# Steps of two layers moved by a slot, dummy matmuls added, and an int4 maximum taken on TensorE, in a four-layer kernel on one core

## The chip, the cores and the metric

The kernel runs on one NeuronCore of a Trainium2 chip. One launch computes all four layers. The metric is the device time of one execution in microseconds. Shorter is better. The core has a matrix engine (PE in the profile, with its weight loads as PEld), a vector engine (DVE), a scalar engine (ACT), a general engine (POOL) and a queue engine (SP) that issues DMAs. Each engine works through its own queue in program order, and semaphores tie the queues together.

## The reference, cut to what matters

The input is 4096 tokens of 128 numbers (16 sequences of 256). Each of four layers normalises x and adds an attention and a feed-forward part of the normalised rows to x.

```python
# layer 0: attention over the 76 keys of highest importance; 8 experts of 512 tokens each
Q, K, V = heads(xn @ wq.T + bq), heads(xn @ wk.T + bk), heads(xn @ wv.T + bv)   # 16 heads of 8
importance = relu(xn @ wi1.T + bi1) @ wi2.T + bi2        # keys outside the top 76 are masked
attn0 = softmax(Q @ K.T / sqrt(8)) @ V @ wo.T + bo
scores = softmax(xn @ wg)                                 # every expert takes its 512 best tokens
top_scores, sel = top_k(scores.T, 512)
routed = xn[sel] * top_scores
ffn0 = scatter_add(sel, (silu(routed @ w1) * (routed @ w3)) @ w2)

# layer 1: sparse causal attention (16 heads of 64), and 8 experts, 2 for each token
# layer 2: attention in learned windows, and a ternary network of width 512
# layer 3: causal attention, 16 heads of 64, S = 256; an int4 linear part with a low-rank part
attn3 = softmax(q @ k.T / 8 + causal) @ v @ Wo + bo
scale = max(abs(kernel)) / 7
w = clip(round(kernel / scale), -8, 7) * scale
ffn3 = xn @ w + bias + (xn @ a) @ b
```

## The kernel before, in words

The 4096 tokens are eight chunks of 512 rows (NC = 8, CT = 512), held as tiles of 128 rows by 128 columns. The order of all instructions is written out by hand: the program is a row of *slots*, and a Python loop says which step of which chunk goes into which slot. A step is a function; a longer step is a generator, and every `yield` in it ends its part in that slot, so one more `yield` moves everything after it one slot later. There is no planner: what is written earlier is earlier in each engine's queue. An engine whose next instruction isn't ready stands still, whatever is behind it.

**PSUM.** The eight accumulator banks are fixed: `sc` is two buffers of two banks (scores, first products, projections), `tp` two single banks (transposes), `mm` and `po` one single bank each. In layer 0, `bank()` hands out `tp`, `tp`, `mm` in turn. A user of a bank waits until the user before has been copied out.

**Layer 0** (`Layer0.run`) has slots -8 to 67, eight for each chunk. In the even slots `exps` forms scores of queries and kept keys in both `sc` buffers on PE (L817), and ACT takes their exponentials (tile `a_p`, L823). In the odd slots `maxima` forms scores of the next chunk in both `sc` buffers (L783), and DVE reduces them (L789); `outputs` multiplies the exponentials of the slot before with the values (L834). `queries`, `divided`, `turned`, `project` and `value` are transposes and small products in between. `prelude` prepares a chunk two chunks ahead.

Beside them runs the routing. `choice` finds for every expert the gate value that keeps 512 tokens: a bitwise search of 15 rounds, one a slot from slot -2, in each of which DVE compares (L485), PE counts with matmuls (L491) and DVE picks. `warm(n)` puts n dummy matmuls of 128x256 in bfloat16 into PE's queue (L373), whose result nobody reads. `expert(e)` starts in slot 19 + 3e: one-hot places on DVE (two slots), indices on PE (`pix`), in the next slot their sums (`eighths`, L605) and four indirect DMAs on POOL that gather 128 rows each (L613), later the product with the gate on DVE (L623), transposes (L629), first products (L638, both `sc` buffers), second products (L648), the copy y on ACT (L653), and four indirect DMAs that add rows to memory (L662). After the last expert eight loads on SP fetch the sums (`fetch`), and POOL adds them to the attention's result (`finish`, L998).

From slot 57 on, `Route.early` normalises layer 0's results for layer 1: `stat` and `root` on DVE, `apply` on ACT and POOL, `turn` (transposes on PE, L1298, and a copy on ACT).

**Layers 1 and 3** share the class `Pipeline`. Its `slots` loop works on one pair of heads u in each slot (128 of them, 16 for a chunk): `scores`, `minima` on DVE, `exps` on ACT, `divide` on POOL (L1145), `transposes` (L1155), `values` (L1169), projections (L1082, L1095; copies on ACT, L1087), and `extra(u)`, a function of the layer. `out_half` is the output projection of 128 rows, nine products into the `mm` bank (L1185, L1187). In layer 3 `norm_steps` normalises the next chunk, beginning in the chunk's slot 3 and ending with four transposes into the `mm` bank (L1059) and a copy on ACT (L1061).

In layer 1 `extra` also carries the chain `route.last`, `route.places` (which place each row has), `scatter` (64 indirect DMAs on POOL), 36 lanes of `blocks` (expert products, L1498 and L1511, with weights gathered by indirect DMA), `gather`, and from slot 56 the generator `aside`, whose end is `quantized`: the int4 weights of layer 3, with the maximum over 128 x 128 numbers.

**Layer 2** (`Layer2.run`) is a loop over chunks with its calls written out; during its last turns `beside(n)` advances layer 3 by n slots.

Of the kernel before, what the change touches and what calls it, by code (L numbers as in the profile page):

```python
# [19 lines left out]
P = 128  # L20
D = 128
# [201 lines left out]
class Layer0:  # L223
# [245 lines left out]
    def choice(self):  # L469
# [9 lines left out]
        for i in range(15):  # L479
# [8 lines left out]
            self.warm(12 if i < 2 else 4)  # L488
# [81 lines left out]
    def expert(self, e):  # L570
# [32 lines left out]
        yield  # L603

# [14 lines left out]
        if e % 2 == 0:  # L619

            yield
# [18 lines left out]
        for hc, p1 in enumerate(p1s):  # L640
            sl = p2.tile([P, CAP], F32, tag="sl", name="sl")
            nc.scalar.activation(sl, p1[:, 0, :], AF.Silu)
            nc.vector.tensor_tensor(g[:, hc, :], p1[:, 1, :], sl, ALU.mult)
        yield
# [235 lines left out]
    def begin(self):  # L880
# [36 lines left out]
        for _ in lane:  # L917
# [6 lines left out]
            -8: [(self.stats, 6, 2, 6), (self.stats, 7, 2, 6), (self.root, 2, 6), (self.apply, 2), (self.apply, 3), warm],  # L924
# [8 lines left out]
    def run(self, tail):  # L933
# [8 lines left out]
        warm = {kk: 5 for kk in range(-8, 4)} | {kk: 2 for kk in range(12, 22)} | {kk: 3 for kk in range(53, 64)}  # L942
        loads = 19 + 3 * NE + 8
        for kk in range(-8, 8 * NC + 4):
# [4 lines left out]
            if 0 <= c < NC and r % 2 == 0:  # L949
                self.exps(c, r // 4, r // 2 % 2)  # L950
# [18 lines left out]
            if kk == 45:  # L969

                self.pg = self.k.po()
# [39 lines left out]
class Pipeline:  # L1011
# [25 lines left out]
    def norm_steps(self, c):  # L1037
# [12 lines left out]
        for t in range(TT):  # L1050
            nc.gpsimd.tensor_scalar(
                xn[:, t, :], x[:, t, :], mv[:, t, 0:1], y[:, t : t + 1], ALU.subtract, ALU.mult
            )
            if t == 1:
                yield
        yield
# [122 lines left out]
    def out_half(self, s, t, wo, first=None):  # L1179

        k, nc = self.k, self.k.nc
        p = k.mm1()
        if first is not None:
            t0 = s % 2 * S + t * P
            nc.tensor.matmul(p[:, :D], lhsT=self.xnT[s // 2][:, t0 : t0 + P], rhs=first, start=True, stop=False)  # L1185
        for n in range(8):
            nc.tensor.matmul(  # L1187
                p[:, :D], lhsT=self.oT[s][:, n, t * P : (t + 1) * P], rhs=wo[:, n, :],
                start=(first is None and n == 0), stop=(n == 7),
            )  # L1190
        return p[:, :D]

    def slots(self, extra, mid=None):

        if self.own:
            yield
            yield from self.norm_steps(0)
            yield
# [55 lines left out]
class Route:  # L1254
# [71 lines left out]
    def early(self):  # L1326

        at = {}
        for first, n in ((0, 2), (2, 2), (4, 2), (6, 1)):
            for c in range(first, first + n):  # L1330
                u = 57 + c + c // 6
                at.setdefault(u, []).append((self.stat, c, first, n))
                for late, step in ((0, self.apply), (1, self.turn)):
                    at.setdefault(59 + c + late, []).append((step, c))
# [6 lines left out]
    def last(self):  # L1341
# [5 lines left out]
        self.apply(c)  # L1347
        yield
# [203 lines left out]
def layer1(k, wk_, w, route, l2, aside, warm):  # L1552
# [15 lines left out]
    def extra(u):  # L1568
# [10 lines left out]
        for g, at, n in ((0, 15, 2), (1, 93, 2)):  # L1579
# [5 lines left out]
        if 0 <= u - 49 < NB // 2:  # L1585
            lanes.append(route.blocks(2 * (u - 49)))
# [26 lines left out]
class Layer2:  # L1613
# [266 lines left out]
    def run(self, wk_, att, begin, l3, route):  # L1880
# [20 lines left out]
        for n in range(NC + 1):  # L1901
# [39 lines left out]
            do(self.turn, q)  # L1941
            do(self.first, f, 3)
            beside(1)
# [27 lines left out]
def quantized(k, pool, a):  # L1971
# [10 lines left out]
    yield  # L1982
    mx = pool.tile([P, 1], F32, name="q_mx")
    nc.gpsimd.partition_all_reduce(mx, m, P, bass_isa.ReduceOp.max)
    yield
# [6 lines left out]
    q = pool.tile([P, D], F32, name="q_q")  # L1992
# [16 lines left out]
def layer3(k, wk_, sh, room, w, xs, out):  # L2009
# [10 lines left out]
    res = {}  # L2020

    def extra(u):
        for late, t in ((9, 0), (13, 1)):
            s, at = (u - late) // 8, (u - late) % 8
            if at or not 0 <= s < 2 * NC:
                continue
            c, n = s // 2, s % 2 * 2 + t
            if n == 0:
                res[c] = k.xp.tile([P, TT, D], F32, tag="x", name="res")
            p = pipe.out_half(s, t, w["o"], first=w["eff"])  # L2030
            nc.vector.tensor_tensor(res[c][:, n, :], p, w["bias"], ALU.add)
            nc.gpsimd.tensor_tensor(res[c][:, n, :], res[c][:, n, :], xs[c][:, n, :], ALU.add)
            if n == 3:
                nc.sync.dma_start(out[c * CT : (c + 1) * CT, :].rearrange("(t p) d -> p t d", p=P), res[c])

# [155 lines left out]
```

## Time and profile before

| what | value |
|---|---|
| median of 3 runs | 1945.82 us (1943.68 to 1952.15) |
| the profiled execution | 1939.03 us |
| its span, first to last instruction | 1937.3 us |
| its mean granted TensorE clock | 0.985 |
| layer 0 | from the start to about 366 us |
| layer 1 | to about 995 us |
| layer 2 | to about 1390 us |
| layer 3 | to the end |

The profile is one execution, recorded by the hardware. The first part of its page gives each engine's busy time, share of the span and number of instructions. The next cuts the span into 40 equal slices of 48.4 us, with one digit each for the busy tenths, and for the clock that PE was granted. A further part follows the chain of work that ended last, from the last instruction back, and gives its shares by engine. Groups and timelines show an instruction as engine, line, operation, output<-input by the program's names, shape and count; in brackets stands the idle time before it and what ended that. In the list of waits a line reads: engine, tile and line, what it waited for, the total in us, the number of times, the longest.

### The profile page before, as it was taken

Reading aid. Unit: us, or ns where it says so; the run is one execution under the profiler, and the core shown is the slowest. Engines: PE = TensorE matmul, PEld = TensorE weight load, DVE = VectorE, ACT = ScalarE, POOL = GpSimd, SP = SyncE. Lnnn points to the kernel's source line nnn. Section 1 sums busy time; section 2 is a strip of 40 time slices with the busy share of each in tenths; the row PEclk is TensorE's granted clock in tenths of the full one; section 3 lists DMA queues with packets and bytes.
Section 4 is the critical chain, followed back from the end, with each engine's and each line's share of the span. In section 5 each row is a group of like instructions: output and inputs, shape, how many; then the busy total and the mean of one; then the engine's idle time right before and its main releaser. Section 6 shows DMA issues by size and latency. Waiting matters only on the chain.

```text
span 1937.3 us, 39257 instructions
## 1 busy us (share of the span) xinstructions
PE 1850.1 (95%) x13823; PEld 1335.7 (69%) x13823; DVE 1226.1 (63%) x4819; ACT 1052.8 (54%) x3162; POOL 960.8 (50%) x1388
## 2 busy tenths in 40 slices
PE   9998889889999899999999999999999999999998
PEld 5555455568878788887754555555577877877786
DVE  6888664697665555568765555443277667766765
ACT  4334545656666566666644444444466666666664
POOL 4015776337997466565664444421144444444442
PEclk9989999899999999999999999999999999999999
DMA  8500223200014354300010000000000000000000
GB/s 248 145 1 13 30 30 66 74 1 23 33 34 129 101 140 136 88 20 15 16 41 5 9 10 12 12 1 1 1 1 8 1 7 7 7 1 7 7 1 12
DMA packets 83208, 72.28 MB, mean 37 GB/s; under 512 B 14466, under 2 KB 74020, under 8 KB 82852
## 3 DMA queue, kind: packets, MB, share of 16 engines
q1 hardware_dynamic: 66784, 38.01, 6.9%
q0 software_dynamic: 15488, 31.61, 6.7%
q8 instruction: 109, 1.79, 0.4%
q14 instruction: 87, 0.71, 0.1%
q10 hardware_dynamic: 740, 0.17, 0.0%
HBM read 49.70 MB, written 24.25 MB: 38 GB/s over the span
## 4 chain that ended last, share of the span: by engine, by line
PE 64%; DVE 7%; POOL 7%; issue 2%; ACT 1%; POOLq 0%; ACTq 0%; DVEq 0%
PE sc L1811 11%; PE sc L1082 9%; PE po L1169 7%; PE tp L1155 7%; PE sc L1110 7%; PE mm L1187 5%; PE sc L1095 4%; POOL e L1145 3%; POOL xb L1452 2%; DVE e L1125 2%; PE po L1511 2%; PE mm L1498 2%; PE mm L1851 2%; DVE eT L1156 1%; PE sc L1803 1%
## 5 line engine op out<-in xcount | busy, mean ns | idle before, releaser
L1145 POOL TENSOR_TENSOR e<-e,rs 128x256 f32<-128x256 f32 (+2 forms) x512 | 400.0, 807 | 483.1 <-DVE rs L1143 448.3
L1136 ACT ACTIVATE e<-e,mn 128x128 f32<-128x128 f32 (+2 forms) x1024 | 442.4, 434 | 285.8 <-DVE mn L1125 281.8
L1156 DVE COPY eT<-tp 128x384 f32<-128x384 f32 x512 | 261.3, 552 | 59.8 <-PE tp L1155 59.6
L1811 PE MATMUL sc<-ff,h 128*128 128x512 f32 x512 | 227.2, 593 | 1.6 <-DVE l_mn L1738 1.6
L1155 PE MATMUL tp<-ident,e 128*128 128x128 f32 x1536 | 219.0, 278 | 8.6 <-POOL e L1145 5.6
L1175 DVE COPY oT<-po 128x512 f32<-128x512 f32 x128 | 88.3, 690 | 215.8 <-PE po L1169 215.8
L1155 PEld LDWEIGHTS tp<-ident,e 128*128 128x128 f32 x1536 | 173.3, 141 | 61.6 <-issue 37.3
L1136 ACT ACTIVATION_READ_ACCUMULATOR e<-e,mn 128x1 f32 x1024 | 191.9, 187 | 0.0
L1811 PEld LDWEIGHTS sc<-ff,h 128*128 128x128 f32 x512 | 94.4, 190 | 106.4 <-issue 101.2
L1125 DVE CUSTOM_DVE_ANT_0 e<-sc,causal 128x128 f32<-128x128 f32 (+1 forms) x512 | 151.8, 353 | 11.2 <-PE sc L1110 10.8
L1125 DVE CUSTOM_DVE_ANT_0 e<-sc,sparse 128x128 f32<-128x128 f32 (+1 forms) x512 | 138.8, 328 | 7.2 <-POOL dist L183 2.2
L1082 PE MATMUL sc<-m,qkv 128*128 128x256 f32 x512 | 126.8, 390 | 1.7 <-DVE mn L1125 1.7
L1691 POOL TENSOR_SCALAR n<-dist,reach 128x128 f32<-128x128 f32 (+1 forms) x128 | 119.2, 931 | 16.4 <-DVE l_mn L1738 5.0
L1187 PE MATMUL mm<-out,oT 128*128 128x128 f32 x1024 | 124.9, 275 | 0.0
L1187 PEld LDWEIGHTS mm<-out,oT 128*128 128x128 f32 x1024 | 119.4, 192 | 0.1
L1790 POOL TENSOR_TENSOR x<-l_o,x 128x256 f32<-128x256 f32 x16 | 11.6, 727 | 199.7 <-DVE l_o L1784 199.3
L1082 PEld LDWEIGHTS sc<-m,qkv 128*128 128x128 f32 x512 | 92.5, 190 | 17.0 <-DVE mn L1125 2.3
L1110 PE MATMUL sc<-n 64*128 64x128 f32 (+1 forms) x1024 | 101.5, 337 | 1.3 <-ACT n L1087 0.8
L1169 PE MATMUL po<-eT,p_v 128*64 128x256 f32 (+1 forms) x1024 | 99.4, 333 | 2.0 <-DVE eT L1156 1.9
L1169 PE MATMUL po<-eT,m 128*64 128x256 f32 (+1 forms) x1024 | 98.1, 332 | 0.4 <-DVE eT L1156 0.4
L1169 PEld LDWEIGHTS po<-eT,p_v 128*64 128x64 f32 x1024 | 63.9, 136 | 43.7 <-issue 16.3
L1742 ACT ACTIVATE p_e<-p_e,l_mn 128x128 f32<-128x128 f32 (+1 forms) x128 | 56.3, 441 | 68.3 <-DVE l_mn L1738 68.1
(433 smaller groups left out, 3686.6 us busy)
## 6 DMA issues: line engine op xcount, KB each, us to landing
xb<-zero SPq DMA_DIRECT2D x1, 4608.0 KB, 20.4
xb<-xb SPq DMA_DIRECT2D x36, 128.0 KB, 2.8
yb<-yb SPq DMA_DIRECT2D x36, 128.0 KB, 2.3
x<-in_L_attn_x SPq DMA_DIRECT2D x8, 256.0 KB, 3.8
m<-in_L_ffn_w SPq DMA_DIRECT2D x8, 256.0 KB, 11.3
xn_d<-x SPq DMA_DIRECT2D x8, 256.0 KB, 8.0
m<-acc_d SPq DMA_DIRECT2D x8, 256.0 KB, 5.4
h<-in_L_ffn_h_wT SPq DMA_DIRECT2D x2, 1024.0 KB, 7.5
```

What stands on the lines that cost most here:

```text
L1082: nc.tensor.matmul(p[:, n, i * S : (i + 1) * S], lhsT=self.wqk[n][:, (2 * gg + i) * P : (2 * gg + i + 1) * P], rhs=(self.xk if n else self ...
L1110: nc.tensor.matmul(ps[:, j, c0:c1], lhsT=qk[r, 0, i, qt * P : (qt + 1) * P], rhs=qk[r, 1, i, k0 : k0 + c1 - c0], start=True, stop=True,)
L1125: nc.vector.tensor_tensor_reduce(out=e[:, j, c0:c1], in0=ps[:, j, c0:c1], in1=self.mask[:, c0:c1], scale=1.0, scalar=3e38, op0=ALU.add, op ...
L1136: nc.scalar.activation(e[:, j, c0:c1], e[:, j, c0:c1], AF.Exp, bias=mn[:, n], scale=-1.0, accum_out=sums[:, n])
L1145: nc.gpsimd.tensor_tensor(e[:, :, c0:c1], e[:, :, c0:c1], bcast(rs[:, 2 * qt : 2 * qt + 2], 2, c1 - c0), ALU.mult)
L1155: nc.tensor.transpose(pt[:, n * P : (n + 1) * P], e[:, j, c0 : c0 + P], k.ident)
L1156: nc.vector.tensor_copy(eT[:, j, :], pt[:, :384])
L1169: nc.tensor.matmul(o[64 * j : 64 * j + 64, t * P :], lhsT=v[:, t ^ self.swap, h : h + 64], rhs=eT[:, j, t * S : t * P + S], start=(t == 0) ...
L1175: nc.vector.tensor_copy(self.oT[s][:, 2 * gg : 2 * gg + 2, :].rearrange("p i s -> p (i s)"), self.po.pop(g))
L1187: nc.tensor.matmul(p[:, :D], lhsT=self.oT[s][:, n, t * P : (t + 1) * P], rhs=wo[:, n, :], start=(first is None and n == 0), stop=(n == 7),)
L1691: self.nc.gpsimd.tensor_scalar(mk[:, j, c0:c1], self.k.dist[:, c0:c1], reach[:, g, t : t + 1], 1e18, ALU.is_gt, ALU.mult)
L1811: self.nc.tensor.matmul(ph, lhsT=self.w[wh][:, c, m * P : (m + 1) * P], rhs=src[c], start=(c == 0), stop=(c == NF - 1))
```

## The change

- **Layer 0, dummies.** 25 instead of 3 in slot -8; in the search 28, 12 and then 7 a round instead of 12, 12 and then 4; 5 instead of 2 in slots 12 to 16.
- **Layer 0, order.** `exps` moves from the head of its slot to behind `project` and `value`. Odd experts take their index sums and gather one slot later, and all experts now have three slots from the gather to the product with the gate (odd ones had two). Second products come a slot later after the first. So an even expert ends one slot later and an odd one three. The loads of the sums leave three slots later. A bank of the dummies is taken in slot 47 instead of 45.
- **Layer 1's rows.** `turn` comes one slot later, for chunks 0 to 6 in layer 0's tail and for chunk 7 in `last`. Scatter, blocks and gather follow one slot later.
- **Layer 3.** `norm_steps` has one more `yield` ahead of its transposes; at the start one `yield` less stands before it. In layer 2 one `beside(1)` moves ahead of `first(f, 3)`. The sum with the bias and x is made on POOL first, for a whole chunk, and PE's result is added to it by DVE. Of the last sequence, seven of nine products of each half are done in slots 126 and 127, in the `mm` and a `tp` bank, and the last two in slot 128.
- **The int4 maximum.** POOL's reduction over the partitions gives way to a copy of each row's maximum to 128 columns (DVE), a transpose into the `mm` bank (PE) and a reduction along the row (DVE).

```diff
@@ Layer0.choice
-            self.warm(12 if i < 2 else 4)
+            self.warm((28, 12, 7)[min(i, 2)])
@@ Layer0.expert
         nc.scalar.activation(fourths, pix[:, :P], AF.Copy)
         yield
+        if e % 2:
+            yield
 
         nc.tensor.matmul(pix[:, P : P + 8], lhsT=fourths, rhs=self.eighths, start=True, stop=True)
...
         yield
         yield
-        if e % 2 == 0:
-
-            yield
+
+        yield
 
         nc.vector.tensor_tensor(
...
             nc.vector.tensor_tensor(g[:, hc, :], p1[:, 1, :], sl, ALU.mult)
+        yield
+
         yield
         py = self.bank()
@@ Layer0.begin
-            -8: [(self.stats, 6, 2, 6), (self.stats, 7, 2, 6), (self.root, 2, 6), (self.apply, 2), (self.apply, 3), warm],
+            -8: [(self.stats, 6, 2, 6), (self.stats, 7, 2, 6), (self.root, 2, 6), (self.apply, 2), (self.apply, 3), (self.warm, 25)],
@@ Layer0.run
-        warm = {kk: 5 for kk in range(-8, 4)} | {kk: 2 for kk in range(12, 22)} | {kk: 3 for kk in range(53, 64)}
-        loads = 19 + 3 * NE + 8
+        warm = {kk: 5 for kk in range(-8, 4)} | {kk: 5 for kk in range(12, 17)} | {kk: 2 for kk in range(17, 22)} | {kk: 3 for kk in range(53, 64)}
+        loads = 19 + 3 * NE + 11
...
-            if 0 <= c < NC and r % 2 == 0:
-                self.exps(c, r // 4, r // 2 % 2)
             if 0 <= c + 1 < NC and r % 2:
                 self.maxima(c + 1, r // 2)
...
             if r >= 6 and 0 <= c + 1 < NC:
                 self.value(c + 1, r - 6)
-            if kk == 45:
+            if 0 <= c < NC and r % 2 == 0:
+
+                self.exps(c, r // 4, r // 2 % 2)
+            if kk == 47:
@@ Pipeline.norm_steps
             if t == 1:
                 yield
+        yield
         yield
         pt = k.mm1()
@@ Pipeline.out_half
-    def out_half(self, s, t, wo, first=None):
+    def out_half(self, s, t, wo, first=None, p=None, upto=8):
...
-        for n in range(8):
+        for n in range(6, 8) if begun else range(upto):
@@ Pipeline.slots
         if self.own:
-            yield
             yield from self.norm_steps(0)
             yield
@@ Route.early
-                    at.setdefault(59 + c + late, []).append((step, c))
+                    at.setdefault(59 + c + 2 * late, []).append((step, c))
@@ Route.last
         self.apply(c)
+        yield
         yield
         self.turn(c)
@@ layer1
-        for g, at, n in ((0, 15, 2), (1, 93, 2)):
+        for g, at, n in ((0, 16, 2), (1, 94, 2)):
...
-        if 0 <= u - 49 < NB // 2:
-            lanes.append(route.blocks(2 * (u - 49)))
+        if 0 <= u - 50 < NB // 2:
+            lanes.append(route.blocks(2 * (u - 50)))
@@ Layer2.run
             do(self.turn, q)
+            beside(1)
             do(self.first, f, 3)
-            beside(1)
@@ quantized
+    q = pool.tile([P, D], F32, name="q_q")
+    nc.vector.tensor_copy(q, m.to_broadcast([P, D]))
+    yield
+    pm = k.mm1()
+    nc.tensor.transpose(pm[:, :P], q, k.ident)
     mx = pool.tile([P, 1], F32, name="q_mx")
-    nc.gpsimd.partition_all_reduce(mx, m, P, bass_isa.ReduceOp.max)
-    yield
+    nc.vector.tensor_reduce(mx, pm[:, :P], AX.X, ALU.max)
     yield
@@ layer3
+        if u == NU - 2:
+            last.append(k.mm1())
+        if u == NU - 1:
+            last.append(k.tp())
+        if u in (NU - 2, NU - 1):
+            pipe.out_half(2 * NC - 1, u - NU + 2, w["o"], first=w["eff"], p=last[-1], upto=6)
         for late, t in ((9, 0), (13, 1)):
             s, at = (u - late) // 8, (u - late) % 8
-            if at or not 0 <= s < 2 * NC:
+            if at or not 0 <= s < 2 * NC - 1:
                 continue
...
                 res[c] = k.xp.tile([P, TT, D], F32, tag="x", name="res")
+                nc.gpsimd.tensor_tensor(res[c], xs[c], bcast(w["bias"], 1, TT), ALU.add)
             p = pipe.out_half(s, t, w["o"], first=w["eff"])
-            nc.vector.tensor_tensor(res[c][:, n, :], p, w["bias"], ALU.add)
-            nc.gpsimd.tensor_tensor(res[c][:, n, :], res[c][:, n, :], xs[c][:, n, :], ALU.add)
+            nc.vector.tensor_tensor(res[c][:, n, :], p, res[c][:, n, :], ALU.add)
             if n == 3:
                 nc.sync.dma_start(out[c * CT : (c + 1) * CT, :].rearrange("(t p) d -> p t d", p=P), res[c])
+        if u == NU:
+            c = NC - 1
+            for t in range(2):
+                p = pipe.out_half(2 * NC - 1, t, w["o"], p=last[t])
+                nc.vector.tensor_tensor(res[c][:, 2 + t, :], p, res[c][:, 2 + t, :], ALU.add)
+            nc.sync.dma_start(out[c * CT : (c + 1) * CT, :].rearrange("(t p) d -> p t d", p=P), res[c])
```

More of the change, by code (lines that the diff above doesn't have):

```diff
@@ L6 @@
 import concourse.tile as tile
-from concourse import bass_isa, mybir
+from concourse import mybir
 from concourse.masks import make_identity
@@ L1177, in values @@
             )
-    def out_half(self, s, t, wo, first=None):
+    def out_half(self, s, t, wo, first=None, p=None, upto=8):
         k, nc = self.k, self.k.nc
-        p = k.mm1()
-        if first is not None:
+        begun = p is not None and upto == 8
+        if p is None:
+            p = k.mm1()
+        if first is not None and not begun:
             t0 = s % 2 * S + t * P
             nc.tensor.matmul(p[:, :D], lhsT=self.xnT[s // 2][:, t0 : t0 + P], rhs=first, start=True, stop=False)
-        for n in range(8):
+        for n in range(6, 8) if begun else range(upto):
             nc.tensor.matmul(
@@ L1991, in quantized @@
     yield
-    q = pool.tile([P, D], F32, name="q_q")
     nc.vector.tensor_scalar(q, kw, inv[:, 0:1], None, ALU.mult)
@@ L2019, in layer3 @@
     pipe = Pipeline(k, wk_, xs, (w["Wq"], w["Wk"]), w["Wv"], k.causal, home=home)
-    res = {}
+    res, last = {}, []
     def extra(u):
+        if u == NU - 2:
[4 more added lines that the diff above has]
+            pipe.out_half(2 * NC - 1, u - NU + 2, w["o"], first=w["eff"], p=last[-1], upto=6)
         for late, t in ((9, 0), (13, 1)):
             s, at = (u - late) // 8, (u - late) % 8
-            if at or not 0 <= s < 2 * NC:
+            if at or not 0 <= s < 2 * NC - 1:
                 continue
```

## The prediction

> **What bounds the kernel now.** I read the page first, then busy time by stretches, then the waits of the stage that loses most, then timelines around each edited place.
>
> ```profile
> PE 1850.1 (95%) x13823; PEld 1335.7 (69%) x13823; DVE 1226.1 (63%) x4819; ACT 1052.8 (54%) x3162; POOL 960.8 (50%) x1388
> PEclk9989999899999999999999999999999999999999
> PE 64%; DVE 7%; POOL 7%; issue 2%; ACT 1%; POOLq 0%; ACTq 0%; DVEq 0%
> ```
>
> PE is busy 95% of the span and holds 64% of the chain that ended last. So an edit pays only where PE is idle or runs at a reduced clock, and costs whatever it adds where PE is full. The clock dips only early. Busy time by stretches places the dips:
>
> ```profile
> 30.00:37.00 7.00, 4.97 (x22) 2.78 (x22) 6.42 (x28) 5.51 (x14) 2.97 (x5) 0.51 0.87 273
> 112.00:119.00 7.00, 7.00 (x45) 5.43 (x42) 3.77 (x11) 1.93 (x2) 0.00 (x0) 0.51 0.00 0
> 347.50:354.30 6.80, 6.78 (x41) 3.23 (x41) 5.94 (x35) 5.02 (x11) 2.07 (x3) 0.50 0.00 0
> 664.90:671.80 6.90, 4.76 (x22) 4.47 (x22) 3.42 (x6) 0.38 (x1) 5.28 (x8) 0.51 0.26 69
> ```
>
> After the stretch and its length come busy time of PE, weight loads, DVE, ACT and POOL, then the granted clock. Each of these runs at half clock, so it can return at most half its length, 3.4 us, and less where another engine is nearly full (DVE 6.42 of 7 in the first).
>
> **Start of layer 0, -1.0 us (-2 to 0).** The 22 added dummies before slot -7's transposes take 0.12 each (17 of them took 2.02 at 57 us), 2.6 us, and PE is idle 3.39 us there waiting for ACT's normalised rows, so they are covered. If they hold the clock in 30 to 37, ACT (5.51 of 7 busy) lets at most 1.5 through.
>
> **Search, -1.0 (-2.9 to +4.6).** Sixteen more dummies in the first round take 1.9 and lie in the 2.3 us that PE waits for DVE's comparison. Three more in 13 rounds cost 0.36 each where DVE waits for PE's count, which it does in 4 of the 15 rounds (4.3 us in all; DVE is busy 54.67 of the 64.5 us): 1.4, or 4.6 if all pay. If the clock holds in 112 to 119, DVE's 2.85 us below its rate of the stretch before (6.62 of 7) come back. I take a little over the middle. The 15 dummies of slots 12 to 16 are covered by DVE, busy 56.76 of 63 us there; without that cover they cost 1.8.
>
> **Experts, 183 to 326 us, -10 (-19 to 0).** The waits of this stage:
>
> ```profile
> ACT y L653 <- DMA acc_d<-y,ids: 11.4, 2, 6.7
> DVE xr L623 <- DMA xr<-xn_d,ids: 10.3, 3, 4.2
> PE sc L817 <- DVE g L643: 5.0, 7, 1.0
> ```
>
> ACT can't write y before the last expert's adds have landed, and what stands behind y on ACT waits too. Four gathers an expert (about 1.25 us each on POOL) and four adds with three memsets (7.5) share POOL's queue, behind the `pick` and `ka` operations. PE inherits these waits three times: 1.77 at 208 (eighths behind ACT), 2.69 at 248 (a bank held until y), 2.08 at 227 (a bank held until DVE, stuck on xr). An odd expert's gather a slot later and two slots more to its product, and second products and adds a slot later for all, put about 12 us (two slots of 6) between gather and use. I take back 6.5, and 3.4 for the two 3.4 us half-clock stretches that follow. The moved `exps`: after first products, PE waits about 1.5 us for the score banks, eight times. Now queries, quotients and projection (0.44 to 1.7 us) go first, hiding some 8 in all. Against it, `maxima` wants the same two banks and must wait for ACT's 1.93 us of exponentials with less work between: 1 us in eight pairs, -8 again. The end at -19 is the second without the bill; at 0 the waits only move.
>
> **Late layer 0, 326 to 366, +1 (-5 to +8).** `exps` last in its slot leaves ACT's 1.93 us bare before `outputs`: the 0.9 us of work moved ahead is lost in each of 8 pairs, 7. The early transposes one slot later remove the 1.34 us at 344.5 and most of the half-clock stretch behind it, together 4; 2 more by filling with expert products, which now end three slots later.
>
> ```profile
> 345.84 1.21 PE L1298 MATMUL tp<-ident,m 128*128 128x128 f32 x4 [1.34 <-ACT m L1292]
> ```
>
> This row shows a 1.34 us idle time, followed by the half clock from 347.5. The Trainium skill ("TensorE: Matmul & The Clock Gate", its table "Why this matters for your kernels") only warns of idle gaps over about 3 us; by that, no dummy or delay here would change the clock, and these terms would be the idle times alone. The row decides: short gaps among thin matmuls suffice.
>
> The eight fetches leave SP three slots later (SP has nothing else then); the first sums on POOL ended at 328 and DVE's statistics began at 335.5, and three slots of 2.3 us use that up: 0 to 3, inside the range.
>
> **Start of layer 1, +1.5 (-2.5 to +4).** PE waited 2.53 us for chunk 7's rows, and the scores after it began at 380.70, released by ACT's copy L1087. ACT is late through the normalisation ahead of it in its queue, which doesn't move. So the idle time stays, the transposes (0.6 at full clock) come later, and a longer idle time may keep the half clock for another 3.4 us. Scatter, blocks and gather move along one slot: nothing else waits.
>
> **The int4 maximum, -5.1 (-6.5 to -3).**
>
> ```profile
> 657.87 0.38 POOL L1984 PARTITION_ALL_REDUCE q_mx<-q_m  x1 [5.76 <-issue]
> 666.01 1.44 POOL L1145 TENSOR_TENSOR e<-e,rs 128x256 f32<-128x256 f32 x2 [7.77 <-issue]
> 666.67 0.47 PE L1155 MATMUL tp<-ident,e 128*128 128x128 f32 x1 [4.78 <-POOL e L1145]
> ```
>
> The operation takes 0.38, but POOL stands still 5.76 before and 7.77 after it without a releaser, around two pool reconfigurations. The division, and PE behind it, wait. The block products L1498 recur every 6.32 us; three periods from 652.57 took 25.09 instead of 18.97: 6.1 us lost, clock included. The replacement's copy and reduction are 0.3 each on DVE, which idles there; the transpose takes the single `mm` bank right after a block's product and waits for ACT to empty it, as L2003 does at 685 (0.5 to 0.7), then 0.3: 1.0. The Trainium skill ("GPSIMD Engine Reference", 4. When to use GPSIMD) calls POOL the only option for a reduction across partitions, which would rule this edit out and make the term 0. PE's own transposes (0.28 each) show that PE can turn the column.
>
> **Layer 2's call order, -1.4 (-1.5 to 0).** The layer 3 transposes now precede `first(f, 3)`, whose matmuls cover ACT's copy out of the `mm` bank:
>
> ```profile
> 1371.09 3.84 PE L1851 MATMUL mm<-f,ff 128*128 128x128 f32 x32 [1.41 <-ACT m L1061]
> ```
>
> **Layer 3's transposes, +4.5 (-5.2 to +8).** They move from the 9th to the 10th slot of a chunk.
>
> ```profile
> 1434.22 0.33 PE L1059 MATMUL mm<-ident,m 128*128 128x128 f32 x1 [0.29 <-POOL m L1051]
> ```
>
> The gain is clear: two waits for POOL, 0.74 us a chunk, 5.2 in seven. But `out_half` runs in that 10th slot and wants the same single bank. In ACT's queue the copy out of it then stands behind exponentials and L1087. In a plain pair (transposes at 1450.60) L1087 ends 4.68 us after the pair began; the copy adds 0.6, so `out_half` starts at about 5.35, against 4.71 now: 0.65 later in 7 chunks. The sum with the bias on POOL (1.25 for four times 0.45) holds DVE until about 1441.9 where its next operation starts at 1442.09: free; without that cover up to 1 us in 8 chunks.
>
> **The end, -1.0 (-2 to 0).** The last two `out_half` leave two products each. POOL's 0.45 and PE's 1.95 go from the chain before the last store at 1931.06, the earlier parts fill 0.54 of idle time and otherwise push the last values back; the copy of oT (0.69) becomes exposed.
>
> **Sum.** -1.0 -1.0 -10.0 +1.0 +1.5 -5.1 -1.4 +4.5 -1.0 = -12.5. The profiled execution took 1939.03 (span 1937.3 and 1.73 outside), so 1926.5 on it. The median of the three runs is 6.8 higher; from it: 1933.3.
>
> **Rivals.** *The waits only move* (experts 0 instead of -10): -2.5, 1943.3. For it: `exps` and `maxima` share two bank pairs, a closed ring with ACT and DVE. Against: the y and xr waits have nothing to do with the banks. *The ring closes on ACT* (slower): in the 18 slot pairs from 28 on, PE stands before `maxima` or `outputs` for most of the 1.93 us plus latency. At 1.3 us a pair beyond what I counted that is 23: +10.5, 1956.3. Below 0.7 it is no loss in all, above 1.23 it is slower by more than 0.5%. For it: 1.1 us of such waits at 329 already; against: lanes put 1 to 2 us between. *Everything pays*: layer 3's collision is hidden and the experts give 16: -28, 1918. *The all-reduce isn't the cause* of POOL's stop would take 5 from the gain; the reconfigurations beside it leave that little room.
>
> **How the numbers follow.** Half a per cent, 9.7 us, is about what a measurement of this kernel can tell from no change. Forecast 0.56 (own range 1926 to 1940), a fifth of it inside 9.7; waits move 0.20; everything pays 0.15; ring 0.09. Faster: 0.45 + 0.15 = 0.60; same: 0.11 + 0.20 = 0.31; slower: 0.09. The range 1918 to 1945 leaves out the ring and the edges.
>
> **What would show it.** Right: no POOL stop near 658; no y or xr waits of 4 us among the experts; clock 1.0 in 30 to 37 and 112 to 119; `out_half` in layer 3 waiting for ACT's L1061 seven times, some 1.6 us each; no 1.41 before L1851. Wrong: PE waits before L783 and L834 on the exponentials over 1 us a pair, or layer 3 shorter by 5.

## The result: slower, and the profile after

The changed kernel takes 1965.66 us (median of 4 runs, 1960.37 to 1977.05) against 1945.44 us for the kernel before: a ratio of 1.0106 with a 95% interval of 1.0076 to 1.0135, so about 20 us slower. The profiled execution took 1970.28 us (span 1968.5), 31.2 us more than the profiled one of before. That is 11 us more than between the medians: executions of one kernel differ by 10 us and more (the changed kernel's by 17), so a difference of a few us between stretches of two profiles can be chance.

The page after, first PE's busy row, then the granted clock in 40 slices, now of 49.2 us each:

```profile
PE 1872.9 (95%) x13916; PEld 1354.8 (69%) x13916; DVE 1227.3 (62%) x4821; ACT 1052.1 (53%) x3162; POOL 957.4 (49%) x1363
PEclk9998879999999999999999999999999999999999
```

PE's share is again 95%, so the page's first part shows nothing. The clock row does: the fourth to sixth slices (148 to 295 us) are at 8, 8 and 7 where all three were at 9. That is, for the most part, the stretch of the experts. Laying the starts of the same steps of the two profiles side by side gives the places, in us of each step from before to after:

| stretch | before | after | difference | predicted |
|---|---|---|---|---|
| start to the exponentials of slot 26 | 170.6 | 174.1 | +3.5 | -2.0 |
| slot 26 to slot 52 (experts) | 150.4 | 178.6 | +28.2 | -10.0 |
| slot 52 to layer 1's first transposes | 61.5 | 61.4 | -0.1 | +1.0 |
| layer 1: its eight slots with the int4 maximum (u = 56 to 63) | 56.6 | 49.6 | -6.9 | -5.1 |
| layer 1: the rest | 557.8 | 562.9 | +5.1 | +1.5 |
| layer 2 | 401.1 | 401.2 | +0.1 | -1.4 |
| layer 3 up to its last transposes | 524.8 | 530.3 | +5.5 | +4.5 |
| from there to the end | 14.5 | 10.4 | -4.1 | -1.0 |

Busy time by stretches (PE, weight loads, DVE, ACT, POOL, then the granted clock). The first two rows are the two dips, in the changed kernel; the next two are the experts' stretch of the table, in the kernel before and in the changed one:

```profile
30.00:37.00 7.00, 5.48 (x33) 2.45 (x31) 6.46 (x27) 5.78 (x15) 3.24 (x5) 1.00 0.87 271
112.00:119.00 7.00, 6.53 (x79) 4.57 (x71) 5.95 (x18) 2.70 (x4) 0.00 (x0) 1.00 0.01 2
170.60:321.00 150.40, 132.05 (x1233) 78.82 (x1232) 92.57 (x204) 78.28 (x108) 99.12 (x102) 0.94 0.21 28
174.10:352.70 178.60, 147.46 (x1225) 91.50 (x1224) 90.99 (x199) 78.01 (x109) 93.33 (x95) 0.86 0.16 22
```

The two dips at the start that the dummies were to close are closed in this profile, as predicted. Among the experts PE stood still for 31.1 us instead of 18.4, and was busy 15.4 us longer with the same work, at a clock of 0.86 instead of 0.94. So PE both stood still longer and ran slower, and the two parts, 12.8 and 15.4, make up the 28.2. The waits between 183 and 360 us after (engine, tile and line, what it waited for: total us, times, longest) say who held it. Line numbers are those of the changed kernel: L612 writes the row numbers `ids`, L656 copies the experts' sums `y`, L792 reduces the maxima `mexp`, L820 is `exps`, L786 is `maxima`, and L826 takes the exponentials `a_p`.

```profile
ACT y L656 <- DMA acc_d<-y,ids: 14.0, 2, 7.5
DVE ids L612 <- DMA acc_d<-y,ids: 13.8, 3, 10.2
PE sc L786 <- ACT a_p L826: 16.1, 16, 5.9
PE sc L820 <- DVE mexp L792: 8.3, 1, 8.3
```

The waits for the xr gathers (10.3 us before) have left the list. The one for `y` has grown from 11.4 to 14.0, and a new one stands beside it: DVE waits for an expert's adds before it may write row numbers. PE has two long waits: 8.3 us once, and one of 5.9 us among sixteen before the maxima, which make 16.1 us against 1.4 before. The timelines of the four engines around the longest wait of DVE:

```profile
235.05 1.65 POOL L665 DMA_INDIRECT acc_d<-y,ids  x1 [0.16 <-issue]
240.73 1.57 POOL L665 DMA_INDIRECT acc_d<-y,ids  x1 [0.19 <-issue]
244.12 0.60 ACT L656 ACTIVATE y<-mm 128x512 f32<-128x512 f32 x1 [6.54 <-DMA acc_d<-y,ids]
244.15 0.16 DVE L612 SCALAR_TENSOR_TENSOR ids<-po,two 128x4 int32<-128x4 f32 x1 [10.20 <-DMA acc_d<-y,ids]
246.50 1.61 DVE L792 TENSOR_REDUCE mexp<-sc 128x4 f32<-128x304 f32 x4
247.40 2.75 PE L820 MATMUL sc<-qa,ka 32*76 32x256 f32 x16 [8.32 <-DVE mexp L792]
```

The first and the last of expert 1's four adds leave POOL at 235.05 and 240.73 us and have landed by 244.1. DVE, which wants to write row numbers, and ACT, which wants to write the next sums, both into buffers that these adds read, stand for this one landing. Behind DVE the places (L576) and the maxima are late, and PE, whose exponentials need the maxima's banks, stands for 8.32 us. The granted clock falls to 0.50 within this stop and stays there for 9.10 us after it.

```profile
242.90:247.40 4.50, 0.00 (x0) 0.00 (x1) 3.25 (x6) 0.60 (x1) 2.00 (x2) 0.50 0.20 29
247.40:256.50 9.10, 9.10 (x85) 6.50 (x89) 5.74 (x12) 2.80 (x4) 7.75 (x9) 0.50 0.25 37
```

PE's other long wait comes from ACT. At 330.69 us ACT, released by the adds of expert 5, at last copies the sums of expert 6, and the exponentials behind it in ACT's queue are late; PE, whose maxima need the banks of these exponentials, stands for 5.93 us:

```profile
330.69 0.60 ACT L656 ACTIVATE y<-tp 128x512 f32<-128x512 f32 x1 [7.51 <-DMA acc_d<-y,ids]
332.34 2.20 PE L786 MATMUL sc<-ka,q 32*128 32x152 f32 x16 [5.93 <-ACT a_p L826]
```

Why the two waits are there can be counted from the code's slots. Row numbers have three buffers (`ids`, bufs=3), so expert e + 3 writes over those of expert e; the sums have one buffer (`y`, bufs=1).

| expert | 0 | 1 | 2 | 3 | 4 | 5 | 6 | 7 |
|---|---|---|---|---|---|---|---|---|
| row numbers written in slot, before | 22 | 25 | 28 | 31 | 34 | 37 | 40 | 43 |
| adds issued in slot, before | 29 | 31 | 35 | 37 | 41 | 43 | 47 | 49 |
| row numbers, after | 22 | 26 | 28 | 32 | 34 | 38 | 40 | 44 |
| adds, after | 30 | 34 | 36 | 40 | 42 | 46 | 48 | 52 |

The sums of an expert are copied in the slot ahead of its adds. Before, adds of expert 1 (slot 31) were three slots ahead of the row numbers of expert 4 (slot 34). After, both are in slot 34; experts 3 and 6 meet in slot 40 in the same way. For the sums the distance is one slot in both kernels, but in another place: before, an odd expert's sums came a slot after an even expert's adds, and the next transposes two slots after the sums (30 and 32); after, an even expert's sums come a slot after an odd expert's adds, and the next transposes in the very next slot (35 and 36).

### The profile page after: what moved, and what is told of

Same layout as the page of the kernel before. It is cut to its first block, busy times and chain, and to the rows that moved or that the text cites. A ratio compares the mean times of both kernels' runs of the same rounds, so it can differ in the third digit from the quotient of the medians.

```text
span 1968.5 us, 39352 instructions
## 1 busy us (share of the span) xinstructions
PE 1872.9 (95%) x13916; PEld 1354.8 (69%) x13916; DVE 1227.3 (62%) x4821; ACT 1052.1 (53%) x3162; POOL 957.4 (49%) x1363
## 4 chain that ended last, share of the span: by engine, by line
PE 64%; DVE 6%; POOL 6%; ACT 2%; issue 1%; ACTq 0%; DVEq 0%; POOLq 0%
PE sc L1818 11%; PE sc L1087 9%; PE po L1174 8%; PE sc L1115 7%; PE tp L1160 7%; PE mm L1194 5%; PE sc L1100 4%; POOL xb L1459 3%; POOL e L1150 2%; PE mm L1505 2%; PE po L1518 2%; PE mm L1858 2%; DVE e L1130 1%; PE sc L1810 1%; PE sc L1811 1%
## 5 line engine op out<-in xcount | busy, mean ns | idle before, releaser
L1087 PE MATMUL sc<-m,qkv 128*128 128x256 f32 x512 | 127.5, 392 | 1.7 <-DVE mn L1130 1.7
L1087 PEld LDWEIGHTS sc<-m,qkv 128*128 128x128 f32 x512 | 92.1, 189 | 17.6 <-DVE mn L1130 2.3
L1115 PE MATMUL sc<-qk 64*128 64x128 f32 (+1 forms) x1024 | 92.1, 320 | 5.7 <-ACT qk L1092 5.7
```

The source lines that it names most:

```text
L1087: nc.tensor.matmul(p[:, n, i * S : (i + 1) * S], lhsT=self.wqk[n][:, (2 * gg + i) * P : (2 * gg + i + 1) * P], rhs=(self.xk if n else self ...
L1115: nc.tensor.matmul(ps[:, j, c0:c1], lhsT=qk[r, 0, i, qt * P : (qt + 1) * P], rhs=qk[r, 1, i, k0 : k0 + c1 - c0], start=True, stop=True,)
```

## The experiments

Theory A was that the row numbers' third buffer is the cause. The rivals were B, the ring of `sc` banks that the late exponentials close on ACT (the slower rival of the prediction), and C, the single buffer of the sums. Ratios are to the kernel before, with 95% intervals. "Experts" is the time from the exponentials of slot 26 to those of slot 52 in the run's profile: 150.4 us before, 178.6 after.

**A fourth buffer for the row numbers.**

```diff
-        ids = p2.tile([P, 4], I32, tag="ids", name="ids", bufs=3)
+        ids = p2.tile([P, 4], I32, tag="ids", name="ids", bufs=4)
```

> The changed kernel with a fourth buffer for the tile of row numbers (ids), nothing else. Theory A, the row numbers: in the changed kernel an odd expert's adds fall into the slot in which the expert three after it writes its row numbers, VectorE stands 10.20 us for them, the pruned logits' maxima wait behind it, and the clock halves; with a fourth buffer that wait is gone, and the time falls by 8 to 20 us from the changed kernel's 1965.7 us, to 1946 to 1958. Theory B, the ring: the late order of the exponentials closes the ring of sc banks on ScalarE; a fourth buffer then changes nothing (within 3 us of 1965.7). Theory C, the new spacing itself: the one buffer of the experts' sums (y), whose release comes with the later adds, holds ScalarE and the ring behind it; a fourth buffer brings at most a third (4 to 8 us).

1962.86 us, ratio 1.0103 (1.0082 to 1.0125); experts 171.9. Theory A alone falls: 3 us came back between the medians, not 8 to 20, and the intervals of the two ratios overlap. By this number B stands; the next runs decide on it. The waits show what took the place of DVE's:

```profile
ACT y L656 <- DMA acc_d<-y,ids: 19.8, 3, 9.2
PE mm L630 <- ACT y L656: 6.3, 1, 6.3
```

DVE no longer stands, but ACT's wait for the same adds grew from 14.0 to 19.8 us. PE now stands 6.3 us in the next slot, before transposes (L630) that want the `mm` bank from which ACT has still to copy the sums.

**The old spacing of the experts, late exponentials kept.** The three `yield` edits of `expert` and the due time of the loads are undone.

```diff
-        if e % 2:
-            yield
...
-        yield
+        if e % 2 == 0:
+            yield
...
             nc.vector.tensor_tensor(g[:, hc, :], p1[:, 1, :], sl, ALU.mult)
         yield
-        yield
...
-        loads = 19 + 3 * NE + 11
+        loads = 19 + 3 * NE + 8
```

> The changed kernel with the experts' old spacing (the three yields of the expert and the due time of the later loads put back); the exponentials stay behind the slot's other work. Theory A and theory C: the adds are early again, so the loss among the experts goes: 1940 to 1948 us, with at most one or two half-clock stretches more than before between 183 and 355 us. Theory B: the ring stays as late as it was, 1955 to 1966 us.

1946.35 us, ratio 1.0007 (0.9990 to 1.0025); experts 152.9. The loss is gone although the exponentials are late. So it belongs to the spacing, and B by itself falls. Yet ACT still waits for the adds:

```profile
ACT y L653 <- DMA acc_d<-y,ids: 15.6, 3, 6.6
PE tp L864 <- ACT y L653: 3.1, 1, 3.1
```

The same kind of wait, 15.6 us in all, costs little here, where the next transposes come two slots later: the one wait of PE behind it is 3.1 us.

**The exponentials back at the head, new spacing kept.**

```diff
+            if 0 <= c < NC and r % 2 == 0:
+                self.exps(c, r // 4, r // 2 % 2)
             if 0 <= c + 1 < NC and r % 2:
                 self.maxima(c + 1, r // 2)
...
-            if 0 <= c < NC and r % 2 == 0:
-                self.exps(c, r // 4, r // 2 % 2)
-            if kk == 47:
+            if kk == 45:
```

> The changed kernel with the exponentials back at the head of the slot (and the later po bank taken at slot 45 again); the experts keep the new spacing. Theory A: VectorE still stands for the adds, 1958 to 1970 us. Theory B: the ring is as before, 1938 to 1946 us. Theory C: as A, 1958 to 1970, since the sums and adds stay late.

1974.62 us, ratio 1.0152 (1.0122 to 1.0181), so it stays slow and is slower by 9 us than the changed kernel: with the new spacing, the late exponentials help. That is some 4 us beyond what A and C expected, and the opposite of B.

**The int4 maximum alone**, in the kernel before.

```diff
+    q = pool.tile([P, D], F32, name="q_q")
+    nc.vector.tensor_copy(q, m.to_broadcast([P, D]))
+    yield
+    pm = k.mm1()
+    nc.tensor.transpose(pm[:, :P], q, k.ident)
     mx = pool.tile([P, 1], F32, name="q_mx")
-    nc.gpsimd.partition_all_reduce(mx, m, P, bass_isa.ReduceOp.max)
-    yield
+    nc.vector.tensor_reduce(mx, pm[:, :P], AX.X, ALU.max)
```

> The kernel before with one edit: the int4 maximum by a transpose and a reduction in place of the all-reduce on POOL. In the changed kernel the period that holds it fell from 56.6 to 49.7 us. If that gain stands by itself: 5 to 7 us faster, 1938.5 to 1940.5. If it only moved (POOL's normalisation or a bank late in the next periods): within 2 us of the kernel before.

1936.13 us, ratio 0.9968 (0.9948 to 0.9989): 2 to 10 us, with 8.5 between the medians and 6.9 in the profile, whose eight slots fell from 56.6 to 49.6 us as in the changed kernel. The gain stands by itself.

**Both buffers.** The first edit, and a second buffer for the sums.

```diff
-        y = p2.tile([P, 4, D], F32, tag="y", name="y", bufs=1)
+        y = p2.tile([P, 4, D], F32, tag="y", name="y", bufs=2)
```

> The changed kernel with a fourth buffer for the row numbers and a second one for the experts' sums (y). The fourth buffer alone left 1962.9 us, so theory A alone has fallen; its trace still shows ScalarE standing 9.24 and 8.05 us for an odd expert's adds before it may write the next sums, 19.8 us in three waits. Theory C (the single buffer of the sums holds ScalarE, the ring and the clock): with a second buffer these waits go, and the time falls to 1940 to 1952 us. Theory D (the spacing itself: the last expert ends three slots later, in slots 48 to 52 that hold only thin work, where the pairs cost 28 us against 12): 1955 to 1963 us.

1944.65 us, ratio 0.9997 (0.9978 to 1.0016); experts 157.4. The time fell by 21 us, the whole excess, with the new spacing still in place, and both waits for the adds have left the list. Theory D falls: the last expert still ends in slot 52. The stretch of the experts is 7 us longer than before all the same. Its row is the first one here; the second is that of a kernel below with the old spacing (the one with the parts that are kept):

```profile
171.80:329.20 157.40, 139.91 (x1229) 85.69 (x1228) 91.73 (x201) 78.73 (x109) 91.57 (x95) 0.90 0.19 25
173.50:330.50 157.00, 138.43 (x1231) 81.04 (x1231) 92.91 (x204) 78.36 (x108) 96.80 (x102) 0.90 0.21 27
```

PE stands still for 17.5 us with both buffers, no longer than the 18.4 of the kernel before, so the 7 us are a lower clock. The kernel with the old spacing shows the same length at the same clock, while the others with the old spacing and the exponentials at the head take 149.7 to 151.5 us. So the 7 us need no new spacing; one profile of each kernel can't say more.

**The sums' buffer alone.**

> The changed kernel with a second buffer for the experts' sums (y) alone; the row numbers keep three. A fourth buffer for the row numbers brought 3 us, both buffers together 21 us. If the sums' buffer is the whole cause: 1943 to 1947 us. If the two waits replace each other (adds that land late hold either VectorE or ScalarE): 1950 to 1962, and VectorE's wait for the adds is still in the trace with 8 to 10 us.

1966.3 us, ratio 1.0105 (1.0084 to 1.0126); experts 171.1. It brings nothing that can be measured in time, and is above both ranges of the expectation, though the wait that the second one named is there. Some of that lies elsewhere: this profile lost 6 us ahead of slot 0 in a half-clock stretch (0.53 from 10 to 20 us) that the profile with both buffers doesn't have. Among the experts its profile is 7.5 us shorter than that of the changed kernel, as with the row numbers' buffer, 6.7. Alone it leaves DVE where it was:

```profile
DVE ids L612 <- DMA acc_d<-y,ids: 14.5, 3, 10.2
PE sc L820 <- DVE mexp L792: 8.3, 1, 8.3
```

7.5 and 6.7 make 14.2, both together make 21.2; these are single profiles, and that of the changed kernel is one of its slower executions. The medians say it more plainly: 3 us for one buffer, none for the other, 21 for both. At expert 1's adds there are two waits for one landing: with the row numbers' buffer alone PE stands 6.3 us for the sums, with the sums' buffer alone 8.3 us for the maxima. The later wait of 5.9 us before the maxima is there without the sums' buffer and gone with it.

**Half of the spacing at a time.** The first kernel has the odd experts two slots later but no extra slot before the second products; the second has that extra slot and no later odd experts. The due time of the loads moves with the last adds (+ 10 and + 9 instead of + 11).

```diff
@@ sums back
             nc.vector.tensor_tensor(g[:, hc, :], p1[:, 1, :], sl, ALU.mult)
         yield
-        yield
@@ odd experts back
-        if e % 2:
-            yield
...
-        yield
+        if e % 2 == 0:
+            yield
```

> The changed kernel with the slot between first and second products taken out again (every expert's sums and adds one slot earlier; the loads with them); odd experts stay two slots later. Theory A (adds in the slot of the row numbers): odd adds now come a slot before the row numbers that reuse their buffer, so VectorE's wait shrinks from 10 to some 3 us: 1950 to 1958. Theory C: an even expert's sums still come one slot behind an odd expert's adds, so the waits for y stay: 1955 to 1966. Theory D: the tail is one slot shorter of three, 1953 to 1960.

> The changed kernel with the two later slots of the odd experts taken out again; the slot between first and second products stays for all. Theory A: the adds come at slots 30, 32, 36 and the row numbers that reuse their buffers at 31, 34, 37, so at most one slot's margin and little wait: 1944 to 1950. Theory C: the order of sums and adds among the experts is the old one, shifted by a slot, so the waits for y are as in the kernel before: 1944 to 1950. Theory D: the tail is one slot longer than before, not three: 1947 to 1953. If the slot between the products is the costly part: 1955 or more.

Sums back: 1956.35 us, ratio 1.0064 (1.0040 to 1.0089), experts 164.9. The ranges of A, C and D all hold it, so it decides nothing among them. Odd experts back: 1967.54 us, ratio 1.0108 (1.0067 to 1.0149), experts 175.0; 14 us or more above what A, C and D expected of it; only the last line of the expectation, that the slot between the products is the costly part, fits. The slots account for both. With the sums back, two pairs have one slot between adds and row numbers, and the next transposes come two slots after the sums that wait. With the odd experts back, three pairs have one slot, and the transposes come in the next slot. The waits, first of the former and then of the latter kernel:

```profile
DVE ids L612 <- DMA acc_d<-y,ids: 5.5, 2, 3.7
```

```profile
DVE ids L610 <- DMA acc_d<-y,ids: 15.5, 3, 8.0
PE tp L629 <- ACT y L655: 6.2, 1, 6.2
```

Two waits and three, as the slots count. PE's single wait of 6.2 us stands before transposes that follow at once; in the former kernel its longest one for `y` is 2.9 us. So one slot of distance is not enough either: the adds leave up to 10 us after their sums (at 235.05 after 224.97 in the changed kernel, POOL having stood 9.11 us for DVE in its `pick`), take 7.3 us to issue and land 2 us later.

**What is kept, without and with buffers.** The kernel before with the int4 maximum, the end of layer 3, layer 2's order and the longer dummies at the start; and the same with both buffers.

> The kernel before with the parts of the change that the traces show to pay: the int4 maximum by a transpose (8.5 us by itself), the end of layer 3 with the bias added early and the last projections begun early (4.1 us in the trace), layer 2's work beside the third products before the first ones (1.7 us), and the longer dummy runs at the start. Spacing, order of the exponentials and layer 3's norm slots as before. Expected 1928 to 1934 us, faster than both kernels; if the parts took from each other, 1935 to 1940.

> The kernel of the parts that pay (int4 maximum, end of layer 3, layer 2's order, dummies at the start; experts and exponentials as before) with the fourth buffer for the row numbers and the second one for the sums. The kernel before stands 11.4 us in two waits of ScalarE for the adds; if they are on the path there too, 1924 to 1931 us against 1935.6 without the buffers; if the rest of the slot hides them, 1933 to 1938.

1935.63 us, ratio 0.9940 (0.9915 to 0.9965), and 1934.09 us, ratio 0.9943 (0.9923 to 0.9963). Both beat both kernels. With the old spacing the buffers bring nothing that can be measured, though ACT's waits for the adds are gone: the 11.4 us of the kernel before were nearly free.

**Layer 3's norm slots alone, and the late exponentials alone**, each in the kernel before. The edits are those of the change to `norm_steps` and `slots`, and to `exps` in `run`.

> The kernel before with the one edit of layer 3's normalisation alone (its transposes a slot later, the slot ahead of the first one taken away). By the prediction's term: a transpose meets out_half in the mm bank once in each of seven chunks at 0.65 us, less at most one slot at the start, so 4 to 5.5 us slower, 1949 to 1950.5, with layer 3's chunks of 16 slots at 67.2 to 67.5 us against 66.6. If out_half is hidden: within 1 us.

> The kernel before with the exponentials behind the slot's other work (and the later po bank taken at slot 47), nothing else. Rival of the ring: sc banks given late to ScalarE, 1.23 us a pair or more over 18 pairs, 8 to 15 us slower. By the runs so far (with the new spacing, late exponentials were 9 us the faster; with the old spacing the trace shows nothing dear): within 4 us of the kernel before.

Norm slots: ratio 1.0010 (0.9995 to 1.0025), so the measurement says no more than -1 to +5 us. The profile is sharper: layer 3 takes 529.2 us to its last transposes against 524.8, +4.4. Late exponentials: ratio 0.9998 (0.9983 to 1.0014), nothing that can be measured; experts 150.4. Rival B has no weight by itself.

**What was still open: start and layer 1.** With both buffers the changed kernel still stood 9 to 11 us above the kernels that keep the paying parts.

> The kernel before with the longer dummy runs alone (25 in slot -8; 28, 12 and 7 in the search; 5 in slots 12 to 16). The prediction gave them -2.0 us. In the profiles so far the exponentials of slot 26 begin at 168.6 to 178.0 us in ten kernels with these dummies and at 168.2 to 172.6 in four without. Theory E (they cost): 2 to 5 us slower than the kernel before, slot 26 at 172 to 175. Theory F (the rest of the change did that): 0 to 2 us faster, slot 26 at 168 to 171.

> The kernel before with the later slots of layer 1's rows alone (chunk transposes, scatter, blocks and gather one slot later). The prediction gave 1.5 us for the start of layer 1 and nothing for scatter, blocks and gather. Traces with these moves take 4.8 to 5.2 us longer from layer 1's first transposes to layer 2. If these moves do it: 3 to 6 us slower, layer 1 at 618.5 to 620.5 us against 614.4. If the late experts did it: within 1.5 us.

> The kernel before with three parts only: the int4 maximum by a transpose, the end of layer 3, layer 2's order; no longer dummies. Under theory E: 1928 to 1934 us, 2 to 5 us below the kernel that has the dummies too (1935.6). Under theory F: 1934 to 1938.

Dummies alone: ratio 1.0006 (0.9989 to 1.0023), slot 26 at 171.9 us. That leaves -2 to +4.5 us, so neither E nor the predicted -2 is excluded, and slot 26 lies between the ranges of E and F. The later slots in layer 1 alone: 1949.44 us, ratio 1.0039 (1.0023 to 1.0055), which is 4 to 11 us; its layer 1 takes 619.8 us against 614.4. So these moves do it, without any late expert. Three parts without the dummies: 1933.25 us, ratio 0.9944 (0.9925 to 0.9962), not to be told from the kernel that has them.

## Why the prediction was wrong, step by step

**The experts: the step that failed.** The prediction put it so: "An odd expert's gather a slot later and two slots more to its product, and second products and adds a slot later for all, put about 12 us (two slots of 6) between gather and use. I take back 6.5, and 3.4". (From gather to product it is one slot more, three instead of two; the product itself comes two slots later.) It was right about the beginning of the chain: the waits for xr went. But it moved the end of the chain too, and did not ask what becomes free there. The row numbers' buffers and the sums' one buffer are released by the adds. Three slots later for an odd expert, the release fell into the slot of the next write. The trace of before had shown one of these waits (`y`, 11.4 us); I counted what PE inherits of it as time to win back, with no count of how many slots its release was from its next use. Instead of -10 the stretch gave +28.2 in the profile. The profile with the two buffers returns 21.2 of it; the other 7 are a lower clock, which a kernel with the old spacing shows too.

**The price of a wait.** Of the 11.4 us for `y` the prediction priced what PE inherits: 2.69 us at 248, as a part of the 6.5. Taking all of them away with the two buffers, in the old spacing, brought 1.5 us between the medians, inside the scatter. In these runs what PE inherits goes with what comes next behind the waiting ACT: with transposes two slots later up to 3.1 us at once, in the next slot 6.2 to 6.3, and 5.9 where exponentials stood behind the copy.

**The rival that went the right way was the wrong one.** The ring of banks was to decide from 1.23 us a pair. Late exponentials alone change nothing, and with the new spacing they helped. The true slower mechanism was not among the rivals. The test named for "wrong", PE standing before maxima and outputs on the exponentials for over 1 us a pair, comes out close and would have misled: 16.1 us before the maxima, 0.9 for each of 18 pairs. But 5.9 of it are one wait behind the sums, and with both buffers 10.4 us of it stay in a kernel that is as fast as the one before. The banks only passed on a wait that began with the adds.

**Start and search, -2.0.** The two dips closed as foreseen (clock 1.00 in both rows above), but the time didn't fall: the changed kernel has a new one of 10 us from 147 us on, and the dummies alone are worth between -2 and +4.5 us. Nor do they hold the clock each time: six of the eleven profiled kernels that have them run at half clock for 3.4 us from 33 or 34 us on. And the kernel with the int4 maximum alone, which has none of them, has a dip of 13.7 us from 145 us on. Why the clock falls there stays open.

**Late layer 0, +1.0.** The sum was -0.1, but by other terms. PE's 4.5 us of waits for normalised rows went, and 5.7 us of waits for ACT's copy of layer 1's projections (L1092 here, L1087 before) stand in their place, most of it once:

```profile
PE sc L1115 <- ACT qk L1092: 5.7, 2, 5.0
```

**The int4 maximum, -5.1.** Right in mechanism and nearly in size: -6.9 in the profile. The replacement's wait for the bank was predicted as 0.5 to 0.7 us, and was 0.47 (PE, in the changed kernel):

```profile
687.69 0.33 PE L1994 MATMUL mm<-ident,q_q 128*128 128x128 f32 x1 [0.47 <-ACT hb L1511]
```

The Trainium skill ("GPSIMD Engine Reference", 4. When to use GPSIMD), by which POOL is the only engine for such a reduction, would have made the term 0. The measurement decides against it.

**Layer 1's slots, +1.5.** The sign was right, the size too small: +5.1 in the changed kernel, +5.4 alone. Of this the first sixteen slots make 3.7 in the kernel with these moves alone (72.9 us against 69.2). They end where the scatter begins, so there the later transposes were priced too low. At u = 88 to 103, around the gather, it takes 67.7 us against 63.5, of which 3.2 is busy time of PE with more instructions (539 against 522), so in part work that has moved in from other slots. "Scatter, blocks and gather move along one slot: nothing else waits" isn't refuted by this and isn't shown either: the parts weren't run one by one.

**Layer 2's order, -1.4.** The wait of 1.41 us before the first products is gone. In the changed kernel layer 2 as a whole is no shorter, 401.2 us against 401.1: 3.4 us of it, from 1055.3 us on, ran at half clock. Three kernels with this order and no such dip (old spacing, sums back, kept parts with buffers) take 399.5 to 399.6 us, so the term holds.

**Layer 3's transposes, +4.5.** Right: the wait of `out_half` for ACT's copy came seven times, as said, at 1.4 us each where 1.6 was said (PE, from 1430 to 1955 us), and the layer is 5.5 us longer, 4.4 with this edit alone.

```profile
PE mm L1192 <- ACT m L1066: 10.1, 7, 1.7
```

**The end, -1.0.** It gave -4.1 in the profile, 3.2 net of 0.9 that the last chunk before it is longer. From the last transposes to the last store it is 6.8 us instead of 8.2, so 1.5 of the 4.1 lie there. The two products left in each half cost PE 1.2 us after the last copy of `oT`, and the copy's exposed part was 0.79, near the 0.69 named. The other 2.6 us lie behind the store, and no term held them. At the program's end POOL runs a closing DRAIN. In the kernel before, the first of its three starts with POOL's last sum and takes 5.97 us, to 1936.5 us, 5.4 us after the store was issued. In the changed kernel POOL has no sums left there, and the DRAIN, from 1953.5 us on, is over before the store leaves at 1964.85. The rows, before and after (times in ns: shortest, median, longest; then first and last start in us):

```profile
L2187 POOLq DRAIN  x3: 52/102/5970, 1930.5 to 1937.0; - x3
L2211 POOLq DRAIN  x3: 51/102/7438, 1953.5 to 1968.2; - x3
```

Put together from the runs, with profile figures where the interval is wider than the term: 21 for the two buffers' waits, 5.4 for layer 1, 4.4 for layer 3's slots, -6.9 for the maximum, -3.2 for the end make +21, and the measured change is 1965.66 - 1945.44 = +20.2. The parts were measured in different company, and the start, layer 2's order and the rest among the experts are left out, so the closeness is partly luck; their order of size is not.

## What to carry to other kernels

Before a step is moved later, list every buffer that its last instruction releases, count the slots to the next write of that buffer, and add the time in which the release is issued and lands; a distance of one slot was too short here. Where two engines stand for the same landing, undoing either one alone can show little, as here, so an experiment that brings nothing doesn't acquit its wait: take both away. A wait in the list is worth only what the engine at the limit inherits from it, and that is read from what stands behind the waiting engine in the next slot.

## What was not expected of the hardware

Four indirect adds of 128 rows each, with three small operations between them, held POOL from 235.05 to 242.3 us, but landed only at 244.1, so a buffer that they read stays taken for about 9 us after the first one leaves. And a stop of 8.32 us on PE cost more afterwards: the clock was 1.00 from 236 to 239 us, and 0.50 for 9.10 us after the stop, in which PE was busy throughout; by estimate some 4.5 us, half of that, were lost besides. The Trainium skill ("TensorE: Matmul & The Clock Gate", "Why this matters for your kernels") warns of idle gaps over about 3 us, and this row agrees; the half clock after 1.34 us that the prediction showed lies outside that rule. That a short gap suffices doesn't follow from its length alone: after the 1.41 us before L1851 in the kernel before, which the prediction shows too, PE was busy from 1371.1 to 1378.0 us at a clock of 1.00.
